# Perceiver block on one core: the first norm's four chunks turned in four banks, with products of ones between them, and the first loads reordered

## The chip, the cores and the metric

The kernel runs on one core of one Trainium2 chip. The time is the device time of one execution in microseconds. A core has five engines with queues of their own: TensorE (PE in the profile; PEld are its weight loads), VectorE (DVE), ScalarE (ACT), GpSimd (POOL) and SyncE (SP). SyncE only issues transfers here; ScalarE and GpSimd issue some too. Engines wait for each other, and for transfers, by semaphores.

## The reference

Sixteen batches go through three blocks, each with a residual: cross attention of the normalised x on a context, causal self attention with low-rank projections and rotary positions, and a mixture of eight low-rank experts with two gates per batch. For this change only the first norm and the scores behind it matter. Everything is float32.

```
def _layernorm(x, axis=-1, eps=1e-05):
    m = jnp.mean(x, axis=axis, keepdims=True)
    v = jnp.var(x, axis=axis, keepdims=True)
    return (x - m) / jnp.sqrt(v + eps)
...
    def _L0_xattn_ref(hidden_states, visual_hidden_state):
        scores = jnp.einsum('bld,bvd->blv', hidden_states, visual_hidden_state)
        probs = jax.nn.softmax(scores, axis=-1)
        return jnp.einsum('blv,bvd->bld', probs, visual_hidden_state)
...
    x = x + _L0_xattn_ref(_layernorm(x, axis=-1), ctx_1024)
    x = x + _L0_attn_ref(_layernorm(x, axis=-1), ...)
    x = x + _L0_ffn_ref(_layernorm(x, axis=-1), ...)
```

x is (16, 128, 512) and ctx_1024 is (16, 2048, 512).

## The kernel before

A batch is one tile of 128 rows by 512 columns. The context of a batch is read twice: as it is (ctx, four transfers of 1 MB) for the values, and turned on the host (ctxT, four blocks of 1 MB) for the scores. Each has four buffers, so a load for the next batch waits until a product has used the block that lies there.

`score(b)` normalises x, turns it into hT (the hidden dimension on the partitions), and multiplies it with the four ctxT blocks: sixteen products of 128x128 for a block, each of which is two passes in the trace[...]. A block's result psc goes from its bank to sc by ScalarE, and VectorE keeps the running maximum mx. Then follow the maximum over the context (tr_m, spread), the exponentials and `attend(b)`, which multiplies them with ctx (av). While the first two batches go through that, the up and down projections are folded into one weight each (fold_v, fold_k, fold_q, turned by tr_fold into w_v, w_k, w_q). Loops over the batches follow, in which the stages of neighbouring batches interleave; the end has an order written out by hand.

The order on TensorE is that of the program: its products and transposes are pinned (`matmul` and `transpose`, lines 137 and 140 in the profile), and so are the loads (line 145). VectorE, ScalarE and GpSimd go through a wrapper (line 115), and their order is chosen by a scheduler except where the program pins it.

At the very start, the order on each queue is:

- SyncE: half of x_0, ctxT blocks 0 and 1 of batch 0, x_1, ctxT blocks 2 and 3, ctx block 0, then the first ctxT block of batch 1, which waits for the products of block 0.
- ScalarE: the other half of x_0, the identity (ident), a table load, and the four copies into hT.
- GpSimd: the tile of ones, the constants, and the two small operations that make the reciprocal root of the first norm.
- TensorE: twelve products of ones with ones ("warm", whose result nobody reads), the four transposes of the first norm, then the score products of batch 0. After the third block come the four transposes of batch 1's norm.

`first_norm` handles the first batch. Statistics are taken of the two halves of x_0 apart and gathered; the norm is written in four chunks of 128 columns, and each chunk is turned by TensorE into its quarter of one bank `tr_1_0` and copied to hT by ScalarE. As all four lie in one bank, the transpose of a chunk waits for the copy of the chunk before it. The second batch (x_1) takes the ordinary norm, with one statistics operation of 512 columns.

PSUM has eight banks in three pools: `ps_tr` with three, `ps_sc` with two for the scores, and `ps_acc` with three. A tile of a pool takes the next bank in turn and waits for the last use of the one that lay there.

Of the kernel before, what the change touches and what calls it, by code (L numbers as in the profile page):

```python
# [11 lines left out]
F32 = mybir.dt.float32  # L12
# [7 lines left out]
P = 128  # L20
B, S, V, D = 16, 128, 2048, 512
# [68 lines left out]
def perceiver_block(ctx: ExitStack, tc: tile.TileContext, io: dict, out: bass.AP):  # L90
    nc = tc.nc

    const = ctx.enter_context(tc.tile_pool(name="const", bufs=1))
# [5 lines left out]
    ps_tr = ctx.enter_context(tc.tile_pool(name="ps_tr", bufs=3, space=PSUM))  # L99
    ps_sc = ctx.enter_context(tc.tile_pool(name="ps_sc", bufs=2, space=PSUM))  # L100
    ps_acc = ctx.enter_context(tc.tile_pool(name="ps_acc", bufs=3, space=PSUM))
# [20 lines left out]
    vector, scalar, gpsimd = InOrder(nc.vector), InOrder(nc.scalar), InOrder(nc.gpsimd)  # L122

    ones = const.tile([P, P], F32, name="ones")
# [3 lines left out]
    ident = const.tile([P, P], F32, name="ident")  # L128
# [7 lines left out]
    def matmul(*args, **kwargs):  # L136
        tc.keep_in_program_order(nc.tensor.matmul(*args, **kwargs))  # L137

    def transpose(*args):
        tc.keep_in_program_order(nc.tensor.transpose(*args))  # L140
# [3 lines left out]
    def load(*args, queue=nc.sync):  # L144
        tc.keep_in_program_order(queue.dma_start(*args))

    queue = nc.sync

    def pinned(ins):
        if not closing:  # L150
            tc.keep_in_program_order(ins)
# [18 lines left out]
    def bank(pool, tag, name):  # L170
        return pool.tile([P, 512], F32, tag=tag, name=name)
# [4 lines left out]
    def mixed(t):  # L176


        return t.rearrange("p (c i q) -> p c q i", c=KC, q=4)

    def plain(t):
        return t.rearrange("p (c q i) -> p c q i", c=KC, q=4)
# [146 lines left out]
    xs, turned_cts, cts = {}, {}, {}  # L329
# [2 lines left out]

    def load_x(b):
        xs[b] = p3.tile([P, D], F32, tag="x", name=f"x_{b}")
        if b:
            load(xs[b], io["x"][b])
        else:

            for cols, by in ((slice(0, D // 2), nc.sync), (slice(D // 2, D), nc.scalar)):
                load(xs[b][:, cols], io["x"][b][:, cols], queue=by)  # L340

    def load_turned(b, vs=range(VC)):
        for v in vs:
            t = p4.tile([P, KC, 512], F32, tag="ctxT", name=f"ctxT_{b}_{v}")
            load(t, io["ctxT"][b, v], queue=queue)
            turned_cts.setdefault(b, []).append(t)
# [10 lines left out]

    def first_norm(x, hT):  # L360

        stats = const.tile([P, 2, 6], F32, name="st_halves")
        mv, rstd = const.tile([P, 2], F32, name="mv_first"), const.tile([P, 1], F32, name="rs_first")
        for half in range(2):
            vector.bn_stats(stats[:, half], x[:, half * D // 2 : (half + 1) * D // 2])
        vector.bn_aggr(mv, stats.rearrange("p n s -> p (n s)"))
        pinned(gpsimd.tensor_scalar_add(rstd, mv[:, 1:2], EPS))
        gpsimd.tensor_tensor(rstd, rstd, mhalf, ALU.pow)
        h = p2.tile([P, D], F32, tag="h", name="h_1_0")
        tr = bank(ps_tr, "tr", "tr_1_0")  # L370
        for c in range(KC):
            at = slice(c * P, (c + 1) * P)
            vector.tensor_scalar(
                mixed(h)[:, c], plain(x)[:, c], mv[:, 0:1], rstd, ALU.subtract, ALU.mult
            )
            transpose(tr[:, at], h[:, at], ident)
            scalar.copy(hT[:, :, c, :], tr[:, at].rearrange("p (a j) -> p a j", a=4))


    def score(b):  # L380

        hT = p1.tile([P, 4, KC, QD], F32, tag="hT1" if b != 1 else "hT3", name=f"hT1_{b}")
        if b:
            h = layernorm(xs[b], f"1_{b}", mix=b == 1)
            yield
            transposed(h[:], hT, f"1_{b}", b == 1)
        else:
            first_norm(xs[b], hT)
            yield
# [597 lines left out]


    load_x(0)
    scalar.dma_start(ident, io["ident"])  # L990

    warm = bank(ps_acc, "acc", "warm")
    for _ in range(12):
        matmul(warm[:, :P], ones, ones, start=True, stop=True)
    load_turned(0, [0, 1])
    load_x(1)
    load_turned(0, [2, 3])
    load_ctx(0, [0])
# [24 lines left out]
    step(score, 1)  # L1023
    step(attend, 0)
    load_x(2)
    step(score, 2, 2)
    load_ctx(1, [0, 1])
# [21 lines left out]
    queue = nc.scalar  # L1049
# [109 lines left out]
```

## Time and profile before

| | us |
|---|---|
| median of 3 runs | 814.68 |
| lowest and highest of them | 813.73, 815.7 |
| the profiled execution | 817.01 |
| its span, first to last instruction | 813.6 |
| TensorE busy in it | 800.7 |

The span begins with the first recorded instruction; what the profiled execution's time has over it lies around it. The page has busy shares by engine, and the span in 40 slices, where a digit gives tenths. The chain of waits follows the last instruction back to what released it, step by step. The table by stages gives each engine's busy time in a stretch, the granted clock of TensorE (1.00 is full), and the transfers. The start of the timeline, with the start and the length of each group in us:

```profile
0.73 0.41 ACTq L145 DMA_DIRECT2D x<-in_x_dram  x1
0.73 0.39 SPq L145 DMA_DIRECT2D x<-in_x_dram  x1
0.99 4.38 PE L137 MATMUL warm<-ones 128*128 128x128 f32 x24 [0.99 <-POOL ones L115]
1.17 0.46 ACTq L115 DMA_DIRECT2D ident<-in_ident_dram  x1
3.49 0.75 DVE L115 BATCH_NORM_STATS2 st_halves<-x 128x6 f32<-128x256 f32 x2 [3.49 <-DMA x<-in_x_dram]
4.28 0.21 DVE L115 BATCH_NORM_AGGREGATE mv_first<-st_halves 128x2 f32<-128x12 f32 x1
5.50 1.17 DVE L115 TENSOR_SCALAR h<-x,mv_first,rs_first 128x128 f32<-128x128 f32 x4 [1.01 <-POOL rs_first L115]
10.40 0.69 DVE L115 BATCH_NORM_STATS2 st<-x 128x6 f32<-128x512 f32 x1 [3.74 <-DMA x<-in_x_dram]
12.31 0.74 DVE L115 TENSOR_SCALAR h<-x,mv,rs 128x512 f32<-128x512 f32 x1 [1.00 <-POOL rs L115]
```

Names carry no buffer numbers: the first `h` is the first batch's, in four chunks, and the second that of batch 1. The bracket is the engine's idle time before the group and what ended it.

### The profile page before, as it was taken

What the parts mean: (1) busy time and instruction counts of PE and PEld (TensorE: products, weight loads), DVE (VectorE), ACT (ScalarE), POOL (GpSimd) and SP (SyncE); (2) the same over time, 40 slices, a digit from 0 to 9 for tenths busy, and PEclk for the clock granted to TensorE, in tenths of its full rate; (3) what the DMA queues carried; (4) which work ended last, traced back from release to release, by engine and by line L of the source; (5) the groups of instructions that cost most, each with busy time, mean ns of one, the idle gap of its engine ahead of it and who ended that gap; (6) DMA issues with size and microseconds to landing.
All of it is one profiled execution on the core that took longest, in us unless ns stands there. A gap on an engine that the chain in (4) does not pass through costs nothing.

```text
span 813.6 us, 14339 instructions
## 1 busy us (share of the span) xinstructions
PE 800.7 (98%) x5524; PEld 567.9 (70%) x5524; DVE 530.6 (65%) x1235; ACT 260.4 (32%) x772; POOL 146.9 (18%) x213
## 2 busy tenths in 40 slices
PE   8999999999999999999999999999999999999996
PEld 7956675868667686775768677576867757686553
DVE  2354839577583956759396675848668594755885
ACT  1223315133241512424152232414223242322452
POOL 1001101212111121211112121121212112121204
PEclk8999999999999999999999999999999999999999
DMA  8999285776949588694967859496794948754102
GB/s 351 389 354 372 102 333 224 290 319 189 400 150 353 215 278 337 197 393 148 353 235 273 343 180 386 154 347 259 246 362 159 385 169 324 285 204 196 41 1 77
DMA packets 77011, 211.04 MB, mean 259 GB/s; under 512 B 6416, under 2 KB 42896, under 8 KB 60560
## 3 DMA queue, kind: packets, MB, share of 16 engines
q10 hardware_dynamic: 15840, 113.45, 35.0%
q1 hardware_dynamic: 57168, 84.62, 29.6%
q0 software_dynamic: 3936, 12.07, 4.4%
q8 instruction: 43, 0.70, 0.3%
q14 instruction: 24, 0.20, 0.1%
HBM read 180.23 MB, written 29.88 MB: 258 GB/s over the span
## 4 chain that ended last, share of the span: by engine, by line
PE 91%; DVE 3%; DMA 2%; POOL 1%; issue 1%; ACT 0%; ACTq 0%; POOLq 0%; SPq 0%; DVEq 0%
PE psc L137 27%; PE av L137 26%; PE v L137 7%; PE k L137 7%; PE q L137 7%; PE o L137 6%; PE pss_sc L137 2%; PE y L137 2%; PE ffn L137 2%; PE pss_acc L137 2%; PE mid L137 1%; DMA ident<-in_ident_dram 1%; DMA there_p<-pX 1%; DMA x<-in_x_dram 1%; DVE att L115 1%
## 5 line engine op out<-in xcount | busy, mean ns | idle before, releaser
L137 PE MATMUL psc<-hT,ctxT 128*128 128x128 f32 x2048 | 237.0, 277 | 0.0
L137 PEld LDWEIGHTS psc<-hT,ctxT 128*128 128x128 f32 x2048 | 233.5, 193 | 0.5 <-issue 0.5
L137 PE MATMUL av<-ctx,sc 128*128 128x512 f32 x512 | 227.3, 596 | 0.0
L137 PEld LDWEIGHTS av<-ctx,sc 128*128 128x128 f32 x512 | 94.4, 190 | 110.5 <-issue 107.9
L115 ACT ACTIVATE att<-att,nmx 128x128 f32<-128x128 f32 x256 | 98.8, 388 | 84.6 <-DVE nmx L115 84.6
L115 POOL TENSOR_SCALAR rs<-mv 128x1 f32<-128x1 f32 x47 | 10.5, 224 | 438.8 <-DVE g_at L115 209.2
L115 ACT COPY sc<-psc 128x512 f32<-128x512 f32 x64 | 37.5, 585 | 141.6 <-PE psc L137 141.6
L115 ACT ACTIVATE sc<-sc 128x512 f32<-128x512 f32 x64 | 40.2, 630 | 90.9 <-DVE sc L115 90.4
L137 PE MATMUL k<-hT,w_k 128*128 128x128 f32 x512 | 60.1, 275 | 0.0
L137 PE MATMUL q<-hT,w_q 128*128 128x128 f32 x512 | 60.0, 275 | 0.0
L137 PEld LDWEIGHTS k<-hT,w_k 128*128 128x128 f32 x512 | 58.5, 192 | 1.5 <-issue 0.8
L137 PE MATMUL v<-w_v,hT 128*32 128x512 f32 x520 | 59.0, 593 | 0.0
L137 PEld LDWEIGHTS q<-hT,w_q 128*128 128x128 f32 x512 | 58.5, 192 | 0.0
L137 PE MATMUL o<-w_c,yT 128*128 128x512 f32 x128 | 57.8, 594 | 0.0
L115 DVE TENSOR_TENSOR mx<-psc,mx 128x512 f32<-128x512 f32 x32 | 21.6, 676 | 49.9 <-ACT sc L115 49.9
L115 ACT ACTIVATE kb<-kT,cst 128x512 f32<-128x512 f32 (+1 forms) x34 | 36.2, 1112 | 39.7 <-DVE kT L115 39.7
L115 ACT ACTIVATION_READ_ACCUMULATOR att<-att,nmx 128x1 f32 x256 | 47.9, 187 | 0.0
L115 DVE TENSOR_SCALAR h<-x,mv,rs 128x512 f32<-128x512 f32 x47 | 27.4, 583 | 31.1 <-POOL rs L115 31.1
L115 DVE TENSOR_TENSOR mx<-psc,sc 128x512 f32<-128x512 f32 x16 | 11.1, 691 | 54.6 <-ACT sc L115 54.6
L115 DVE TENSOR_TENSOR sc<-sc,spread 128x512 f32<-128x512 f32 x64 | 42.6, 672 | 3.3 <-PE spread L137 3.3
L115 DVE TENSOR_TENSOR att<-att,rsm 128x512 f32<-128x512 f32 x64 | 43.4, 678 | 0.8
L115 DVE TENSOR_REDUCE nmx<-att 128x4 f32<-128x512 f32 x64 | 41.9, 672 | 0.1
(139 smaller groups left out, 859.1 us busy)
## 6 DMA issues: line engine op xcount, KB each, us to landing
ctx<-in_ctx_dram ACTq DMA_DIRECT2D x56, 1024.0 KB
ctxT<-in_ctxT_dram ACTq DMA_DIRECT2D x52, 1024.0 KB
there_p<-pX SPq DMA_DIRECT2D x28, 512.0 KB
pT<-there_p SPq DMA_DIRECT2D x28, 512.0 KB
ctxT<-in_ctxT_dram SPq DMA_DIRECT2D x12, 1024.0 KB
there<-blocks SPq DMA_DIRECT2D x42, 256.0 KB
hT<-there SPq DMA_DIRECT2D x42, 256.0 KB
ctx<-in_ctx_dram SPq DMA_DIRECT2D x8, 1024.0 KB
```

Of the source, the lines that this page charges most:

```text
L115: ins = issue(*args, **kwargs)
L137: tc.keep_in_program_order(nc.tensor.matmul(*args, **kwargs))
```

## The change

Five edits, all at the start of the program:

- x_0 comes in one transfer on SyncE's queue; ScalarE's queue begins with the identity.
- The statistics of x_0 are one operation of 512 columns.
- Each of the four chunks is turned into a bank of its own: the first in `ps_acc`, the others in `ps_tr`.
- After each chunk's transpose and copy, one product of ones is issued.
- There are fifteen products of ones at the start instead of twelve.

```diff
     def load_x(b):
         xs[b] = p3.tile([P, D], F32, tag="x", name=f"x_{b}")
-        if b:
-            load(xs[b], io["x"][b])
-        else:
-
-            for cols, by in ((slice(0, D // 2), nc.sync), (slice(D // 2, D), nc.scalar)):
-                load(xs[b][:, cols], io["x"][b][:, cols], queue=by)
+        load(xs[b], io["x"][b])
...
     def first_norm(x, hT):
 
-        stats = const.tile([P, 2, 6], F32, name="st_halves")
+        stats = const.tile([P, 6], F32, name="st_first")
         mv, rstd = const.tile([P, 2], F32, name="mv_first"), const.tile([P, 1], F32, name="rs_first")
-        for half in range(2):
-            vector.bn_stats(stats[:, half], x[:, half * D // 2 : (half + 1) * D // 2])
-        vector.bn_aggr(mv, stats.rearrange("p n s -> p (n s)"))
+        vector.bn_stats(stats, x)
+        vector.bn_aggr(mv, stats)
...
         h = p2.tile([P, D], F32, tag="h", name="h_1_0")
-        tr = bank(ps_tr, "tr", "tr_1_0")
         for c in range(KC):
+
+            tr = bank(ps_tr, "tr", f"tr_1_0_{c}") if c else bank(ps_acc, "acc", "tr_1_0_0")
             at = slice(c * P, (c + 1) * P)
...
-            transpose(tr[:, at], h[:, at], ident)
-            scalar.copy(hT[:, :, c, :], tr[:, at].rearrange("p (a j) -> p a j", a=4))
+            transpose(tr[:, :P], h[:, at], ident)
+            scalar.copy(hT[:, :, c, :], tr[:, :P].rearrange("p (a j) -> p a j", a=4))
+            warm_up(1)
...
     warm = bank(ps_acc, "acc", "warm")
-    for _ in range(12):
-        matmul(warm[:, :P], ones, ones, start=True, stop=True)
+
+    def warm_up(n):
+        for _ in range(n):
+            matmul(warm[:, :P], ones, ones, start=True, stop=True)
+
+    warm_up(15)
```

## The prediction

> **What bounds the kernel now.** I read the page first: TensorE against the other engines, and its granted clock.
>
> ```profile
> PE 800.7 (98%) x5524; PEld 567.9 (70%) x5524; DVE 530.6 (65%) x1235; ACT 260.4 (32%) x772; POOL 146.9 (18%) x213
> PE   8999999999999999999999999999999999999996
> PEclk8999999999999999999999999999999999999999
> ```
>
> TensorE is busy from the second to the last but one slice of 20.3 us. Time can therefore be won only where it is idle or slow, and the change touches only the first slice, where both rows show an 8. The chain of waits over the first 40 us says what holds it there:
>
> ```profile
> 0.73 0.41 ACTq L145
> 1.17 6.05 DMA ident<-in_ident_dram
> 7.35 0.39 PE tr L140
> 7.77 0.27 ACT hT L115
> 8.09 0.49 PE tr L140
> 8.60 0.27 ACT hT L115
> 9.74 0.48 PE tr L140
> 10.22 12.71 PE psc L137 x96
> 22.93 0.44 PE tr L140 x4
> ```
>
> The identity is issued at 1.17 us and is the last thing the first transpose waits for, at 7.3. Then each transpose waits for ScalarE's copy out of the one bank (0.83 us per chunk). From 10 us on it is score products without a gap. But 96 passes (48 products, two passes each[...]) take 12.71 us, while a later stretch of the same products (32 passes in 3.57 us) gives 0.112 us a pass, or 10.7 for 96. A table by stages of 3.41 us shows why:
>
> ```profile
> 0.63:4.04 3.41, 3.05 (x14) 3.05 (x15) 0.55 (x2) 1.28 (x1) 1.19 (x4) 1.00 0.60 198
> 4.04:7.45 3.41, 1.43 (x13) 1.27 (x12) 1.58 (x6) 0.00 (x0) 0.80 (x2) 1.00 1.04 421
> 7.45:10.87 3.42, 2.35 (x9) 1.50 (x9) 0.47 (x1) 1.06 (x4) 0.00 (x0) 0.50 1.03 424
> 10.87:14.28 3.41, 3.41 (x17) 3.41 (x17) 1.15 (x3) 0.00 (x0) 0.79 (x2) 0.50 1.01 420
> 14.28:17.69 3.41, 3.41 (x32) 3.41 (x32) 0.00 (x0) 0.58 (x1) 0.00 (x0) 1.00 1.03 365
> ```
>
> The first pair of figures after the length is TensorE's busy time; the last three columns are granted clock, DMA share and GB/s. The clock is 0.50 from 7.45 to 14.28 and 17 passes fit where 32 do later. (In the first row the warm-up passes also take 0.213 us each until 4.04 and 0.112 after it, so there too the array ran at half speed, whatever the column says.) After 10 us TensorE waits for no transfer in the first 120 us.
>
> [...]the 64 KB identity, behind half of x on ScalarE's queue, shares the engines with the 1 MB loads of SyncE's queue and is seen 6.05 us after its issue.[...]
>
> **The change part by part.** *Identity first on ScalarE's queue, x in one transfer on SyncE's.* The identity is issued at 0.73 instead of 1.17, beside x, ahead of the large loads. The halves of x issued at 0.73 had the first statistics start at 3.49; x in one transfer is the same 256 KB with half as many packets, the identity adds 64 KB. I take 3.49 for x and no wait for the identity; bounds −0.2 and +0.6 us. The loads behind x on SyncE keep their order, and ScalarE loses one issue of 0.41 us.
>
> *Statistics.* One of 512 columns (0.69, the row of x_1) and one gathering (0.18) replace two of 256 (0.75 together) and one (0.21). On x_1, statistics to the start of the normalised row took 12.31 − 10.40 = 1.91 us; in the first norm 5.50 − 3.49 = 2.01. So h starts at 5.40 and its first chunk is done at 5.40 + 0.39 = 5.79, 5.86 with a signal; the next ones follow by 0.26.
>
> *15 warm-up products for 12.* The 24 passes end their issue at 5.21 (last start 5.10 + 0.112). Six more at 0.112 give 5.88: they end as the first chunk arrives, and cost nothing.
>
> *Four banks and products between.* No transpose waits for a copy. Each turn is one transpose pass (0.11; four took 0.44 at 22.93) and one product of two passes (0.22): 4 × 0.335 = 1.34, so score products start at 5.88 + 1.34 = 7.22. The products of ones are 0.9 us on the path; without them VectorE's 0.26 a chunk would set the pace, so they cost some 0.4 net, and buy the clock. The seventh score pass needs the last copy: the transpose at 6.88, about 0.36 to the copy's start, 0.27 the copy, 0.05 signal give 7.56; the pass comes at 7.22 + 6 × 0.112 = 7.89. Hidden, with 0.3 to spare. The first score block landed at 6.38 (its sixteen completions in the packet records), so about 6.7 with the signal latency seen for x: 0.5 to spare.
>
> *The clock.* From 4.04 on TensorE now never pauses for more than some 0.1 us, so the window to 7.45 is full instead of 1.43 of 3.41, and the clock stays. 4.27 us at half (10.01 to 14.28) hold 20 passes, which take 2.23 at full: 2.04 us won. The start goes from 10.01 to 7.22: 2.79 won. Sum 4.83 for windows lying as in this profile.
>
> *What is late next.* All loads were issued by releases that TensorE gives (the second batch's block is issued when the first block has been used, at 15.82), so they move with it. Even if none moved, the tightest, the third score block of batch 1, lands at 29.34 and would be wanted at 34.42 − 4.83 = 29.6. It does move: a release at 14.3 instead of 19.4 closes the two holes in the transfer rate at 17 and 20 us. I cost it at nothing, at most 0.4.
>
> *The rest of the program.* In the compiled order SyncE, GpSimd and ScalarE are otherwise unchanged; VectorE's order changes where the weights are folded (55 to 70 us): the copy folded_k of the first half goes ahead of the statistics of x_2, and those of x_2 wait there for its transfer. TensorE stood 0.44 us at 63.15 for just that copy; the next copy now stands behind h_2, about 0.25 late, and a bank 0.2. Net nothing, bounds −0.45 and +0.5. Banks of the two pools rotate by one and two places; each tile still waits for the third before it.
>
> The sum against the profiled execution: it ran 817.0 us, span 813.6 and 3.4 around it; less 4.8 is 812.2. Its windows lay badly for it, though. Sliding the boundaries by tenths of a window and redoing the sum[...], the 96 passes of before end between 21.2 and 22.8 us (profile: 22.8), mean 21.9[...]; those of the changed kernel end between 17.9 and 18.8, mean 18.2, because a later rise leaves more warm-up passes at 0.213. The gain over placements is 3.0 to 4.9, mean 3.7. The runs shown, 813.73 to 815.7 with median 814.68, are below the profiled one and spread by two us, which fits. I take 3.9 off 814.7, between the mean and this profile: **810.8 us**.
>
> **The rivals.** *The clock falls all the same.* If products of ones count for little, or gaps at the waits are larger, the half clock runs to 10.9 or 14.3 with score products in it. To 14.3 it costs (14.28 − 7.45)/2 = 3.4 of the 4.8: gain 1.4, 813.3 us. For it: 1.43 of 3.41 was not enough to hold it. Against: 2.35 of 3.41 near the end (806.17 to 809.58) was, and the new window holds nearly 3.4.
>
> *A transfer takes the place of the identity.* If x in one piece lands 0.6 later, or the identity shares its time, everything to the seventh pass moves: gain 3.3, 811.4; with the first score block late too, 1.5 lost in all, 812.3. For it: the transfers are the only thing at 90% and more there. Against: the identity adds only 64 KB ahead of the first block, beside 256 KB of x, which are there in both.
>
> *Slower: VectorE blocks on x_2 while the weights are folded.* [...]behind the statistics of x_2 stand w_v and the next folded_k, for which TensorE waits. x_2 landed at 56.4; VectorE would come to it at about 61.5 − 4.8 = 56.7. It costs nothing until 56.7, and one for one after. It eats the gain of 3.9 from a landing at 60.6, and gives 0.2% slower, 816.4, at 62.2. For it: there are only 0.3 us to spare if x_2 doesn't move. Against: its queue is released by TensorE's own products, which come earlier.
>
> **How the numbers follow.** Forecast 0.77, clock 0.10, transfer 0.10, blocked 0.03. The forecast's own range is 809.5 to 812.0 (gain 2.7 to 5.2, the placements and the fold's bounds); the transfer case lies at its top, and the range for 8 in 10 is 809.4 to 812.5. A measurement tells about 0.2% (1.6 us) from no change: faster means under 813.05. The forecast and the transfer case lie there, and nearly half of the clock case (0.06 kept): 0.93; the rest of the clock case 0.04; slower 0.03.
>
> **What would show it.** Identity and x landed by 3.5; h from 5.4; transposes from 5.9, each followed by two passes; score products from 7.2; granted clock 1.00 to the end once it has risen; 96 passes in 10.7 us; the next batch's transposes near 18. Wrong would be a stage at 0.50 after 4 us, a wait of TensorE for ctxT or x, or a stall longer than 0.5 near 58 us.

## The result, and the profile after

The changed kernel takes 811.03 us (median of 6 runs, 810.36 to 811.16) against 814.70 before (6 runs, 813.63 to 815.70): ratio 0.9954, interval 0.9941 to 0.9967, a gain of 3.7 us. The profiled execution took 810.97 us with a span of 809.2; before, the span was 813.6.

The page first, the rows that answer to those of before:

```profile
PE 800.2 (99%) x5538; PEld 568.5 (70%) x5538; DVE 529.7 (65%) x1234; ACT 260.4 (32%) x772; POOL 146.6 (18%) x213
PE   9999999999999999999999999999999999999996
PEclk9999999999999999999999999999999999999999
```

The 8 in the first slice is gone from both rows. TensorE's busy time has hardly moved (800.7 to 800.2), although 14 passes were added: what went was idle time and half-speed time. The chain of waits at the start (start and length in us, then what held the end up):

```profile
0.99 5.35 PE warm L137 x30
6.34 0.21 PE tr L140
6.55 0.22 PE warm L137 x2
6.78 0.11 PE tr L140
...
7.44 0.11 PE tr L140
7.55 0.22 PE warm L137 x2
7.77 10.72 PE psc L137 x96
18.49 0.44 PE tr L140 x4
```

The 6.05 us of the identity and the ScalarE copies are no longer in it. TensorE works without a real pause from 0.99 us, and the 96 passes take 10.72 us instead of 12.71, that is 0.112 each. The chain gives ends of work; by their starts the first transpose is at 6.22 (7.35 before), the first score pass at 7.61 (10.01), and the second batch's transposes at 18.33 (22.77). The granted clock changes in steps in the traces: it is 0.50 from 7.45 to 14.28 before (6.83 us), from 799.97 to 803.39 here and from 7.86 to 11.28 in the banks-only kernel below (3.42 each). A stretch of 3.41 or 3.42 us counted from a change of the clock in the same trace is called a window here, as in the prediction; the first rise of the clock is read from the warm-up passes, which go from 0.213 to 0.112 us each there (4.67 in the changed kernel, 4.04 before).

The table by stages, where the last three columns are granted clock, DMA share and GB/s (even stretches of 3.40 us here, not windows of the clock):

```profile
7.30:10.70 3.40, 3.40 (x33) 3.40 (x32) 0.63 (x1) 0.49 (x2) 0.00 (x0) 1.00 1.02 422
10.70:14.10 3.40, 3.40 (x33) 3.40 (x33) 0.99 (x3) 0.59 (x1) 0.80 (x2) 1.00 1.02 431
```

The stage at 0.50 is gone here. Another has appeared 800 us later, in the table by stages at the end, this time cut at windows of the clock:

```profile
796.56:799.97 3.41, 1.16 (x8) 0.97 (x8) 2.33 (x5) 0.37 (x1) 2.89 (x5) 1.00 0.28 79
799.97:803.39 3.42, 3.31 (x10) 2.23 (x11) 1.58 (x3) 0.59 (x1) 1.64 (x2) 0.50 0.24 77
```

And in the timeline of TensorE there (start, length of the group):

```profile
800.99 1.92 PE L137 MATMUL ffn<-wb,mid 128*128 128x512 f32 x2
802.70 1.39 PE L137 MATMUL mid<-hT,wa 128*128 128x128 f32 x8
```

One window at the end had TensorE busy for only 1.16 of 3.41 us (it waits there for the gathered expert weights), and in the next one the clock is half. The two passes of ffn take 1.71 us from their start to that of mid. In a run without that stage (the kernel without products between, below) ffn starts at 800.52 and mid at 801.64, 1.12 us.

So the profiled spans differ by 4.43 us as follows, by the starts of marked instructions in both traces: 4.44 won by the second batch's transposes at 18.33; 0.40 where the weights are folded (first fold_v to first v: 13.88 before, 13.48 after); 0.38 in the loop (first v to the last pass of o: 730.77, 730.39); 0.79 given back at the end (from there to the end: 13.18, 13.97).

### The profile page after: what moved, and what is told of

It reads as the page before. It is cut to its first block, busy times and chain, and to the rows that moved or that the text cites. A ratio compares the mean times of both kernels' runs of the same rounds, so it can differ in the third digit from the quotient of the medians.

```text
span 809.2 us, 14363 instructions
## 1 busy us (share of the span) xinstructions
PE 800.2 (99%) x5538; PEld 568.5 (70%) x5538; DVE 529.7 (65%) x1234; ACT 260.4 (32%) x772; POOL 146.6 (18%) x213
## 4 chain that ended last, share of the span: by engine, by line
PE 97%; DVE 1%; POOL 0%; issue 0%; ACT 0%; POOLq 0%
PE psc L137 28%; PE av L137 28%; PE k L137 7%; PE q L137 7%; PE v L137 7%; PE o L137 6%; PE pss_sc L137 2%; PE y L137 2%; PE ffn L137 2%; PE pss_acc L137 2%; PE mid L137 2%; PE warm L137 1%; PE tr_m L140 0%; PE tr L140 0%; PE spread L137 0%; PE lg L137 0%
## 5 line engine op out<-in xcount | busy, mean ns | idle before, releaser
L137 PEld LDWEIGHTS o<-w_c,yT 128*128 128x128 f32 x128 | 23.9, 196 | 23.8 <-issue 23.0
```

## The experiments

All times are medians; each has runs of the kernel before beside it on its chip, whose median was 814.70 for the changed kernel and 815.20 to 815.48 for the others. The ratio is the recorded estimate over all runs, not exactly that of two medians. "tr" and "psc" are the starts of the first transpose and of the first score pass in the profiled execution, "second" is the start of the second batch's transposes.

| kernel | us | ratio to before, interval | tr | psc | second |
|---|---|---|---|---|---|
| changed kernel | 811.03 | 0.9954, 0.9941 to 0.9967 | 6.22 | 7.61 | 18.33 |
| loads only | 811.83 | 0.9957, 0.9940 to 0.9973 | 6.35 | 8.64 | 19.36 |
| banks only | 811.84 | 0.9953, 0.9934 to 0.9971 | 8.18 | 9.06 | 20.89 |
| more products only | 813.63 | 0.9981, 0.9974 to 0.9988 | 8.43 | 11.04 | 21.75 |
| changed, none between | 810.60 | 0.9941, 0.9925 to 0.9958 | 6.48 | 7.16 | 17.93 |
| changed again | 811.17 | 0.9944, 0.9927 to 0.9960 | 7.34 | 8.67 | 19.39 |
| none between, tail filled | 810.16 | 0.9936, 0.9917 to 0.9954 | 7.31 | 7.94 | 18.76 |
| none between, x in halves | 811.82 | 0.9952, 0.9935 to 0.9968 | 6.23 | 8.84 | 19.63 |
| both of these | 811.36 | 0.9947, 0.9930 to 0.9964 | 6.87 | 8.40 | 19.19 |
| two between | 811.79 | 0.9961, 0.9948 to 0.9974 | 6.24 | 8.46 | 19.18 |
| twelve, none, tail | 811.20 | 0.9945, 0.9932 to 0.9959 | 5.98 | 6.91 | 17.64 |
| changed and tail | 811.03 | 0.9953, 0.9935 to 0.9971 | 6.80 | 8.13 | 18.85 |
| twelve, one, tail | 810.07 | 0.9945, 0.9926 to 0.9965 | 6.14 | 7.47 | 18.19 |

**One part at a time: the loads.** The kernel before, with the load order and the single statistics of the changed one:

```diff
-            for cols, by in ((slice(0, D // 2), nc.sync), (slice(D // 2, D), nc.scalar)):
-                load(xs[b][:, cols], io["x"][b][:, cols], queue=by)
+        load(xs[b], io["x"][b])
```

> The kernel before with only the new order of loads and the single statistics: one bank, twelve warm-up products, none between. Theory (start and clock are two separate terms): the identity is there before h, so the transposes run from about 6.2 us; each still waits for the copy before it (0.66 us a turn at full clock, 0.83 at half), so score products start near 8.3 instead of 10.0; TensorE is idle most of 5.2 to 8.3, so a stage at 0.50 stays. The first 96 passes end between 19.1 and 20.8 us, time about 813.3 us, gain 1.4. Rival (the late identity is the whole story): nearly the full gain, 811.5 or less.

Measured: a gain of 3.4 us (2.2 to 4.9 by the interval), far more than the 1.4 of the theory; by the median it is a little less than the rival wanted, but the interval leaves room for it. The turns were as expected (0.68 us each, score passes from 8.64), but the clock was not:

```profile
3.13:6.54 3.41, 3.41 (x17) 3.23 (x16) 1.52 (x5) 0.00 (x0) 0.80 (x2) 1.00 1.01 404
6.54:9.95 3.41, 2.34 (x16) 1.76 (x16) 0.53 (x3) 1.06 (x4) 0.00 (x0) 1.00 1.01 420
9.95:13.36 3.41, 3.41 (x33) 3.41 (x33) 1.63 (x3) 0.59 (x1) 0.80 (x2) 1.00 1.01 425
```

The clock stays at full after a window in which TensorE was busy for 2.34 us; before, it fell at 7.45 after one with 1.43. In this execution the earlier start by itself shortened the pause, and the clock did not fall: start and clock are not two separate terms. The other three runs have a mean clock of 0.997 or 0.998 and spans 0.8 to 1.1 us longer; where they were slow, no trace shows.

**The banks alone.** The kernel before, with only the four tiles of the change in place of one.

```diff
-        tr = bank(ps_tr, "tr", "tr_1_0")
         for c in range(KC):
+            tr = bank(ps_tr, "tr", f"tr_1_0_{c}") if c else bank(ps_acc, "acc", "tr_1_0_0")
...
-            transpose(tr[:, at], h[:, at], ident)
+            transpose(tr[:, :P], h[:, at], ident)
```

> The kernel before with only the four banks: x in halves, identity second on ScalarE's queue, twelve warm-up products, none between. Theory: the transposes still begin at 7.3 when the identity lands, but no copy stands between them, so score products start near 7.8; the pause from 5.2 to 7.3 lets the clock fall for one window in some placements. The first 96 passes end between 18.5 and 20.2, time about 812.3, gain 2.5. Rival (the late identity is the whole story): the start moves little, gain under 1.

Measured: a gain of 3.4, above the theory's 2.5, though the interval (2.4 to 5.4) just takes that in; "the late identity is the whole story" falls. With a bank for each chunk no transpose waits for a copy: from the first transpose to the first score pass it is 0.88 us (8.18 to 9.06), against 2.66 before (7.35 to 10.01). In this execution the identity came even later than in the profile of before (first transpose at 8.18 instead of 7.35), and the clock fell for one window only, from 7.86 to 11.28:

```profile
4.45:7.86 3.41, 1.12 (x10) 0.93 (x9) 1.19 (x5) 0.00 (x0) 0.80 (x2) 1.00 1.02 420
7.86:11.28 3.42, 3.10 (x14) 3.01 (x15) 0.88 (x2) 0.91 (x4) 0.07 (x1) 0.50 1.02 422
```

After 3.10 of 3.42 us busy the clock rose at 11.28; after the 2.35 of 3.42 before the change, at 10.87, it did not.

**More products of ones alone.** 22 instead of 12 at the start, and two after each transpose of the kernel before:

```diff
-    for _ in range(12):
-        matmul(warm[:, :P], ones, ones, start=True, stop=True)
+    warm_up(22)
...
             scalar.copy(hT[:, :, c, :], tr[:, at].rearrange("p (a j) -> p a j", a=4))
+            warm_up(2)
```

> The kernel before with only more products of ones: 22 at the start, until the identity lands, and two after each transpose, inside the wait for the copy; one bank, loads as before. Theory: the score products start near 9.8 as before, but the clock doesn't fall after its first rise; 96 passes take 10.7 us and end near 20.7 to 21.7; time about 813.8, gain 1.0. Rival (the array needs real work or a longer run to hold the clock): a stage at 0.50 stays after the rise, and the time is that of before, 814.7.

Measured: 813.63, as the theory had it, with no stage at 0.50 after the rise at 6.10. Products whose result nobody reads held the clock here: before, without the added ones, it fell at 7.45. Score passes began only at 11.04, since the 44 passes (24 of 0.213 up to the rise, 20 of 0.112 after it) go on until 8.43, the start of the first transpose; even so the kernel gains.

The gains of the three parts alone are 3.4, 3.4 and 1.6, those of the whole 3.7 to 4.0: they overlap, and the first two each take away much of the same idle time and half-speed time. Some 0.4 us of these two gains lies elsewhere, where the weights are folded (see below); the third has none of that.

**The changed kernel without products between the chunks.**

```diff
             scalar.copy(hT[:, :, c, :], tr[:, :P].rearrange("p (a j) -> p a j", a=4))
-            warm_up(1)
```

> The changed kernel without the products of ones between the chunks. Rival (they hold the clock, as the prediction said): a stage at 0.50 follows the first rise and the time is 1 to 2 us above the changed kernel's, 812 to 813. Theory formed from its trace (the gap they fill is only 0.15 us a chunk, so the clock holds without them): no stage at 0.50 before 100 us, score products start near 7.1 instead of 7.6, time 0.5 us below the changed kernel's, 810.5.

Measured: 810.60, and the clock is full from its rise at 5.28. VectorE begins h at 5.76 in both traces. First the changed kernel, then the one without the products:

```profile
5.76 1.18 DVE L115 TENSOR_SCALAR h<-x,mv_first,rs_first 128x128 f32<-128x128 f32 x4 [1.01 <-POOL rs_first L115]
7.61 10.88 PE L137 MATMUL psc<-hT,ctxT 128*128 128x128 f32 x96
```

```profile
5.76 1.17 DVE L115 TENSOR_SCALAR h<-x,mv_first,rs_first 128x128 f32<-128x128 f32 x4 [1.01 <-POOL rs_first L115]
7.16 2.11 PE L137 MATMUL psc<-hT,ctxT 128*128 128x128 f32 x17
```

The score passes come 0.45 us earlier without them. (From the first transpose it is 0.68 instead of 1.39, but that is not their price: the clock rose 0.6 us later here, so the warm-up lasted longer and held the first transpose back to 6.48.) The rival, which was the prediction's own reason for these products, falls for this execution, and the four other traces of kernels with none between, below, show no stage at 0.50 at the start either (rises at 4.76, 5.47, 6.11 and 7.05).

**The changed kernel with two between.**

```diff
-            warm_up(1)
+            warm_up(2)
```

> The changed kernel with two products of ones after each transpose instead of one. Theory (they lie on the path and buy no clock): four turns of 0.56 us instead of 0.33, so score products start 0.9 us later than in the changed kernel for the same start of the transposes; time 812.0. Rival (they hold the clock in some placements, so that more of them is worth something): 811.2 or less.

Measured: 811.79, near the theory's 812.0. From the start of h to the first score pass it is 1.40, 1.85 and 2.77 us with none, one and two. The second product of a chunk costs its 0.22 us four times; the first costs half of that, since without it TensorE would wait for VectorE's next chunk (0.25 to 0.26 us apart in the trace with twelve and none). The medians, 810.60, 811.03 and 811.79, go the same way, though their intervals overlap.

They also hold something else. All five runs with two between have a mean clock of 0.997 or 0.998, and the profiled one has a window at half clock near the end:

```profile
789.85:793.26 3.41, 3.05 (x46) 2.53 (x46) 2.81 (x15) 2.16 (x6) 1.06 (x1) 1.00 0.02 5
793.26:796.68 3.42, 3.42 (x5) 1.35 (x5) 2.92 (x14) 0.29 (x2) 2.60 (x3) 0.50 0.47 102
```

The last eight passes of o take 5.38 us there, against 3.68 in the kernel with none between. TensorE was busy for 3.05 us in the window before, mostly with small products (lg with 8 output columns, tr_row with one element, and y), and yet the clock fell: in the kernel before it rose at 4.04 after a window with the same 3.05. Recorded busy time alone does not tell the two apart.

**The changed kernel again, for its scatter.**

> The changed kernel as it is, for its time beside the next three on one chip. Theory (windows placed by chance fall on the end of the program too): a part of its runs, about two in three as in the six runs so far, has a stage at 0.50 in the last 14 us and is 0.5 to 0.9 us longer than the others; spans near 808.7 without and 809.3 with it. Rival (that scatter is something else): no such split.

Measured: spans of 809.5, 809.7 and 809.3 at a mean clock of 0.998, and 808.8 at 1.0. With the first six, seven of ten runs are at 0.997 or 0.998 (809.2 to 809.7) and three at 1.0 (808.6 to 808.8), the split of the theory. In the two traces the window at half is at the end, as it says (799.97 and 798.99); for the other five the mean clock alone speaks. The profiled one also shows the other side of the placement, at the start:

```profile
0.28:3.69 3.41, 2.70 (x12) 2.70 (x13) 0.12 (x1) 1.28 (x1) 1.34 (x8) 1.00 0.58 192
3.69:7.10 3.41, 3.41 (x18) 3.41 (x17) 1.93 (x6) 0.00 (x0) 0.80 (x2) 1.00 1.02 407
```

The clock did not rise after 2.70 of 3.41 us busy but at 7.10, so nearly all of the thirty passes ran at half speed, the warm-up lasted to 7.3, and the transposes began at 7.34 though h's first chunk was there by 5.9.

**The end of the program filled, x in halves, and both.** Ten products of ones in the hand-written order of the end, and for the second kernel x in halves on two queues with the identity behind the first half on SyncE:

```diff
+    named(y, fill=lambda: fill(7))
+    named(z, fill=lambda: fill(3))
...
+            load(xs[b][:, : D // 2], io["x"][b][:, : D // 2])
+            load(xs[b][:, D // 2 :], io["x"][b][:, D // 2 :], queue=nc.scalar)
+            load(ident, io["ident"])
```

> The changed kernel without products between the chunks, and with ten products of ones at the end of the program: seven after the last projection, where TensorE waited 2.5 us for the expert weights, and three before the last batch's expert product. Theory: the clock no longer falls in the last 14 us whatever the placement; no run below a mean clock of 1.0 apart from the few us after the last product; the upper runs of the kernel without them (808.6 to 809.0) come down to about 808.0, median 809.9. Rival (they delay the products behind them, or the dip costs nothing): median 810.6 or more.

> The changed kernel without products between the chunks, with x in halves on two queues again and the identity behind the first half on SyncE's queue, ahead of the large loads. Theory (x in one piece is what made h 0.26 later than the prediction took it): statistics start near 3.5 instead of 3.84, h at 5.5, transposes at 6.0 unless the warm-up products are still running, score products 0.25 earlier; time 0.0 to 0.3 below that of the kernel with x in one piece, 810.4. Rival (the first score block, pushed back by the identity, is then what is late): a wait of TensorE for ctxT, no gain.

> Both edits of the two kernels beside it. Theory: the gains add, since one lies in the first 8 us and the other in the last 14: median near 809.6. Rival: the earlier start is lost again at the tail; no better than the kernel with the tail filled alone.

Measured: the filled tail has two runs with spans of 807.9 and 808.0, which is what the theory promised, the profiled one at 808.8 (a late rise, at 7.05, as above; its end has no stage at 0.50), and one at 810.0, at a mean clock of 0.998, that it did not foresee. The rival is in part right, too: six passes of the filling, 0.67 us, stand in the chain of waits between the products ffn and mid. From the last pass of o to the end this trace and those of the three kernels with a filled end below take 13.11 to 13.17 us. Without the filling it is 12.67 to 12.77 where the clock stayed full there (four traces), and 13.19 to 13.97 with a window at half (three). So in these traces the end with the filling is some 0.4 us longer than one at full clock without it, and up to 0.8 shorter than one with a window at half. With x in halves the rival wins. The timeline:

```profile
6.23 0.95 PE L140 MATMUL tr<-ident,h 128*128 128x128 f32 x4
8.84 0.35 PE L137 MATMUL psc<-hT,ctxT 128*128 128x128 f32 x1 [1.66 <-DMA ctxT<-in_ctxT_dram]
```

The first score block is what TensorE waits for, 1.66 us. In the packet records its last completion comes at 8.39, against 6.29 in the changed kernel, although its issue moved back only from 1.18 to 1.65. Both edits together have the same wait (0.93; last completion at 7.93) and by the medians were slower than the filled tail alone, though the intervals overlap.

The profiled execution of "both" is also one of the long ones (span 811.4; its other three runs 809.4 to 809.6), and shows why. VectorE's last results end at 806.8 there and at 806.1 in the changed kernel; from there to the end it is 4.7 us instead of 3.1. The transfers in that stretch, first of "both", then of the changed kernel (queue, kind: packets, MB, share of 16 engines):

```profile
q1 hardware_dynamic: 288, 0.26, 24.1%
q8 instruction: 1, 0.02, 2.7%
```

```profile
q1 hardware_dynamic: 288, 0.26, 24.5%
```

A fetch of 16 KB of instructions, 1.4 us long in the packet records, runs on one DMA engine from 807.3 to 808.7, amid the last output transfer, whose last packet then ends 3.0 us after the last result instead of 1.4: from 808.72, when the fetch is over, its last sixteen packets of 1 KB run one after another. Every one of the fourteen traces has such a last fetch, at some time from 793 to 816 us; in this one alone it falls into the last output.

**Twelve at the start, and the products between once more.** The first has twelve products at the start, none between and the filled end; the second is the changed kernel with the filled end; the third is the second with twelve at the start.

```diff
-    warm_up(15)
+    warm_up(12)
```

> Twelve warm-up products instead of fifteen, none between the chunks, and the ten products at the end of the program; loads, statistics and banks as in the changed kernel. Theory[...]: with late windows the fifteen products run at half speed and end at 7.3, after h; twelve end at 6.1 at the latest, and the clock holds all the same, since the pause before the transposes is under 1.1 us. Score products start by 7.4 in every placement; median 809.7, 0.4 below the same kernel with fifteen. Rival (the shorter warm-up lets the clock fall in some placements): a stage at 0.50 after the first rise in some runs, those above 811, median 810.2 or more.

> The changed kernel, its products between the chunks kept, with the ten products of ones at the end of the program. In the kernel with twelve warm-up products and none between, three runs of five were 1.8 us longer than the other two at a mean clock of 0.998, the price of one window of score products at half speed. Theory (the products between keep the clock in the placements in which the pause alone would let it fall): no run with such a step, all spans within 1.1 us from 808.0 to 809.1 at a mean clock of 1.0, median 810.3. Rival (fifteen at the start are enough, the ones between only cost 0.45): steps of 1.8 in neither, but slower than the fifteen-and-none kernel by 0.45, median 810.6 or more.

> The same with twelve warm-up products instead of fifteen. Theory (the products between keep the clock): no run has a step of 1.8 us; spans near 808.1 in all placements, since the transposes never wait for the warm-up; median 809.9. Rival (it is the length of the warm-up that keeps the clock): part of the runs at 809.8 or more with a mean clock of 0.998, median 811.

Measured: the first has spans of 807.6 and 807.8, and three of 809.4 to 809.5. I took that step for the clock at the start. The second and third speak against it: with products between, two of six runs each are still 1.1 to 2.5 us above the others (810.4 and 810.6 against 808.9 to 809.3; 810.1 and 810.5 against 808.0 to 808.4). Both theories about the start fall on these steps. In the five kernels with a filled end, nine of 25 runs are such; in ten runs of the changed kernel and four of the one with none between, no run is (the one with two between has two of five at 811.0 and 811.1 against 809.5 to 810.0, at a lower mean clock). The instruction fetch at the end is shown for one of the nine, and its size fits. For the other eight there is no trace. Three of them (one of "twelve, none, tail" and two of "twelve, one, tail") have a mean clock of 0.999; a whole window of 3.41 us at half would give 0.998 (an estimate: half of 3.41 us, 1.7, is 0.002 of a span of 809), so in these the step is no such window. Why a filled end should meet the fetch more often (the added products shift where a fetch falls) is only argued.

Without such a step twelve products are better than fifteen, as the late placements say: 808.0 to 808.4 with one between, against 808.9 to 809.3. By medians the twelve-one-tail kernel (810.07) and the none-between-tail kernel (810.16) are the lowest, but their intervals overlap with that of the changed kernel: no version is shown to beat it.

## Why the prediction was right

The time, 810.8 predicted and 811.03 measured, came out by the mechanism that was named, with several terms off that cancel.

*Identity and statistics.* The identity no longer holds anything, as predicted. x was taken to arrive as before (statistics at 3.49); in one transfer it arrived at 3.84 in the profile, and at 3.39 to 3.98 in the eight other profiles with that order, inside the bound of 0.6. The chain behind it was right: 5.76 − 3.84 = 1.92 us from statistics to h, predicted 1.91.

*Warm-up and turns.* A turn is 0.33 to 0.34 us after the first one (0.39), as predicted, and the first score pass comes 1.39 us after the first transpose (1.34). The start at 7.61 instead of 7.22 has two causes, either of which would have brought most of it: x came 0.35 later, so h's first chunk was done at 6.17, and the clock rose at 4.67 instead of 4.04, so the warm-up, too, went on to 6.18 instead of 5.88. The copies and the first score block were hidden, as said.

*The clock.* It held, and 96 passes take 10.72 us (10.7). But the reason given for the products between, that they "buy the clock", is not what the runs show: without them it held as well, in all five traces. Their price, "some 0.4 net", was right for the reason given: it measured 0.45, and in the trace with twelve and none the transposes start 0.25 to 0.26 us apart, VectorE's pace.

*Placement of the windows.* This step was right in kind: the first rise of the clock lay between 4.04 and 7.10 us in the profiles. By what rule a window gives full clock was an assumption of mine that no trace shows, and the prediction's own table speaks against it: after the window from 7.45, with 2.35 of 3.42 us busy, the clock stayed at 0.50. The sums over placements, with their mean gain of 3.7, rest on it and are not shown. What the traces do show, window by window: at half clock, 2.65 us busy (the filled tail) and 2.70 (the changed kernel again) were not followed by a rise, 3.05 (before) and 3.10 (banks only) were. At full clock, 1.12 (banks only), 1.16 (the changed kernel) and 1.43 (before) were followed by a fall, 2.34 (loads only) was not. Nor was 1.68, near the end of the kernel before:

```profile
799.35:802.76 3.41, 1.68 (x4) 0.38 (x2) 2.91 (x10) 0.29 (x1) 2.80 (x3) 1.00 0.51 147
802.76:806.17 3.41, 2.03 (x13) 1.66 (x14) 2.33 (x4) 0.49 (x2) 2.99 (x6) 1.00 0.12 46
```

The window of small products with two between (3.05, and a fall) does not fit in with these, so they give no rule. A rise as late as 7.05 or 7.10 occurred in two traces (the filled tail, the changed kernel again), and thirty passes then lasted to 7.3. What made up for that in the sum is not shown. The kernel before may also be slower than I had it: with the same loads the first transpose waited for the identity until 8.18 in the banks-only run, while I used 7.35 for all. That the 3.9 I took comes so near the measured 3.7 (2.7 to 4.8 by the interval) is in part luck.

*Where the weights are folded.* "Net nothing" was wrong by 0.4, within its bound: the stall went and neither of the two feared ones came. In the chain of waits of the kernel before and of the changed one:

```profile
61.77 1.13 PE fold_k L137 x16
...
62.92 0.59 ACT folded_k L115
...
63.59 0.63 PE tr_fold_k L140 x4
```

```profile
57.32 1.02 PE fold_k L137 x16
58.34 1.02 PE tr_fold_k L140 x8
```

Before, TensorE has to stop within the transposes of folded_k, for a copy; after, it goes on. The chain names ScalarE's copy, done at 63.50; VectorE's copy of the other half of folded_k ends beside it, at 63.44, and the other traces point to that one. From the first fold_v to the first v it is 13.47 us in the kernels with the loads only and the banks only, as in the changed one, and 13.89 in the one with more products only, as before. In the first three VectorE makes its first copy folded_k ahead of the third batch's h, in the other two behind it. So these 0.4 us go with the order that the scheduler chose, and not with the earlier start.

*What was not foreseen* is the end. In seven of ten runs the mean clock says that it fell for a window, for some 0.6 us by the spans, and both traces have that window at the end. That moving the program forward makes this more frequent is not shown: none of the 50 runs of the kernel before beside the experiments has a mean clock of 1.0, and half clock near the start, as in its trace, would hide what its end does.

The 0.38 us in the loop does not go with the change. It is one step in one batch, near 588 us in the trace of before: the chain of waits goes there through ScalarE's own load issues to its operation mid (588.46) and from that to the product ffn (588.88), where in the changed kernel it stays on TensorE. The kernel with none between has the same step near 727 us, and 730.75 in the loop; nine traces, the changed kernel's among them, have 730.39 or 730.40.

In the profiled pair, then, the start gave 4.44 of the predicted 4.83, and the three other terms (0.40, 0.38 and −0.79) cancel by chance.

Of the rivals, the clock that falls all the same did not occur at the start, the transfer in place of the identity occurred as 0.35 us of x (and in full once the identity was put ahead of the score blocks, in the experiment with halves), and VectorE was never blocked on x_2.

## What to carry to other kernels

Idle time of TensorE at the start was paid twice here, once as idle time (the first score pass at 10.01, and at 7.61 without it) and once as half clock for the real products behind it (96 passes in 12.71 us, and in 10.72 without it); so removing either of two causes of idleness, the loads or the shared bank, brought most of the gain (3.4 us each, of 3.7 to 4.0 for the whole), and the gains did not add. Filler products were not free here: of those between the chunks the first cost half its length (0.45 of 0.88 us over four chunks) and the second all of it (0.92), those at the end cost 0.4 us, and thirty passes at half speed became the bound itself (to 7.3, with h's first chunk there by 5.9). When a gain of a few us is measured, compare the two traces part by part to the end: here three parts far from the change, each of 0.4 to 0.8 us, happened to cancel.

## What the runs showed of the hardware

- At half clock, windows of 3.41 to 3.42 us with 3.05 us (before) and 3.10 us (banks only) of recorded TensorE time were followed by full clock; those with 2.35 (before), 2.65 (filled tail) and 2.70 (changed kernel again) were not. At full clock, windows with 1.12 (banks only), 1.16 (changed kernel) and 1.43 (before) were followed by half clock; those with 1.68 (before) and 2.34 (loads only) were not. One of small products, at full clock with 3.05, was followed by half clock (two between).
- The placement of the windows differs between the executions profiled: the first rise lay at 4.04 (before), 4.45 (banks only), 4.67 (changed kernel), 5.28 (none between), 6.10 (more products only), 6.54 (loads only) and 7.10 us (changed kernel again), though TensorE started at 0.99 in each. Of two executions of the changed kernel, the one with the rise at 4.67 began the score passes at 7.61, the one with 7.10 at 8.67.
- With a 64 KB transfer ahead of it on the same queue, the first 1 MB block landed at 8.39 (x in halves) and 7.93 (both of these) in two executions, against 6.29 in the changed kernel and 6.38 before, with its issue 0.47 us later. What takes the rest is open.
- In one execution (both of these) a 16 KB instruction fetch of 1.4 us lay within the last output transfer, whose last packet ended 3.0 us after the last result, against 1.4 in the changed kernel.
